# The last of 28 outer products: one inner product leaves PSUM by itself, the last two swap, and the result is stored in halves

## The chip, the cores and the metric

The kernel runs on one core of a Trainium2 chip. The metric is device time in microseconds (us) of one execution; for the kernel before, three runs gave a median of 528.67 (528.14 to 529.69). A separate execution was profiled; lower is better.

## The reference, cut to what matters

`x` holds 64 sequences of 64 tokens, 1024 wide, so 4096 tokens. Two residual layers follow each other.

```python
# layer 0: a low-rank adapter picked by sequence (rank 16)
x = x + einsum('bnr,bor->bno', einsum('bni,bri->bnr', x, B[ids0]), A[ids0])
# layer 1: a dense product and two of eight low-rank experts by token
base   = einsum('btd,od->bto', x, W)
logits = einsum('btd,ed->bte', x, Wr) + 5.0 * one_hot(ids1)
gates  = softmax of the two largest logits, spread over the eight experts
lora   = einsum('bter,bte,eor->bto', einsum('btd,erd->bter', x, A1), gates, B1)
x = x + base + 2.0 * lora
```

All is float32. The kernel adds the identity to W, so that the second residual comes out of the dense product, and works on transposed arrays: `outT` is 1024 outputs by 4096 tokens.

## The kernel before, in words

**Two levels of a product by sevenths.** The dense product takes most of the time. The tokens are cut into eight blocks of 512, and two neighbouring blocks, `ka` and `kb`, make one of four rounds (`s` = 0 to 3, `NSUP` is 4). In a round, the 1024 x 1024 weight matrix and the tokens of the two blocks are each seen as 2 x 2 quarters, and the product of the two is formed from seven products of quarters and sums of them, in place of eight (the method of Strassen and Winograd). These seven are the *outer products*, numbered 1 to 7 and worked in the order `ORDER = (1, 2, 6, 7, 5, 3, 4)` (line 247); the last outer product of the kernel is thus n = 4 of round 3. Each outer product is again formed from seven *inner products*, called p1 to p7 here. Except for two outer products of round 0, all go this way.

**An inner product.** `product(n, ps, k, start)` (line 833) issues four matmuls of 128 x 128 weights by 256 tokens into one PSUM tile of 128 x 2 x 256[...]. For n and k both out of 2, 3, 4 and 7, two more matmuls add the expert part from `b1_sb`. Each float32 matmul shows as two instructions in the profile, so an inner product has 8 or 12 rows there.

**Banks.** Two PSUM tags, `a` and `b`, have two banks each. Within an outer product, p1, p6, p5 and p3 accumulate in one bank of tag `a` (`("pa", s, n)`), in this order; p2 has a bank of tag `b` for itself; p7 and p4 share a further bank of tag `b` (`("pb2", s, n)`).

**How results leave.** The inner sums of this method have terms in common, so a bank is read while it is still being accumulated: `leave(n, ps, i, cs, js, more)` (line 866) reads the bank in its current state and writes it into row half `i` and token half `j` of the outer product's result, in SBUF. Without `more` it adds a stored base (`U` or `V`, sums of earlier outer products; where there is none, ScalarE copies), with `more` it adds to what is there. For n = 4 all are additions on VectorE (DVE) of 128 x 512 elements, with `V` as base. In `step` (line 940), p7 does not leave at once: after p5 there are two additions into the same place (row half 1, token half 1), one of the bank of p1 + p6 + p5 and one of p7's bank. Later p4 is accumulated onto p7, and p4 + p7 is added at row half 1, token half 0.

**The order of the inner products.** The loop in `products` (lines 962 to 986) calls, for each outer product, p1, p2, p6, p7, p5, and keeps p3 and p4 as `rest`, which are put among the first steps of the next outer product: the third after its p1, the fourth after its p2. The last outer product of a round has no successor, so its `rest`, p3 and then p4, ends the round.

**Stores.** `done(n, i, cs, js)` (line 892) is called after p2, p5, p3 and p4, when one token half of one row half is complete. It counts the halves of a row half in `left`; when the second is there, it plans one transfer of the row half, 256 outputs by 512 tokens, 512 KB, on SP's queue.

**What sets the order.** Steps are added to a `Plan` (line 34) with an engine, an estimated duration, what they read and write, a due time `at` and the PSUM or SBUF slots that they take. `Plan.order` runs a simple model of the engines and picks, of the steps that could start first, the one with the smallest due time. The resulting list is issued in that order on each engine, and is not rearranged afterwards. Semaphore waits are put in by the framework, for a PSUM bank by the whole tile: a matmul that writes a bank waits until an earlier read of it is over.

Of the kernel before, what the change touches and what calls it, by code (L numbers as in the profile page):

```python
# [14 lines left out]
P = 128  # L15
# [162 lines left out]
def kernel(  # L178
# [52 lines left out]
    TB = 512  # L231
    NBLK = NT // TB
    NSUP = NBLK // 2
# [5 lines left out]
    QO = O // 4  # L239
    HT = TB // 2  # L240
# [6 lines left out]
    ORDER = (1, 2, 6, 7, 5, 3, 4)  # L247
# [5 lines left out]
    act, pool, sp = Pinned(tc, nc.scalar), Pinned(tc, nc.gpsimd), Pinned(tc, nc.sync)  # L253
# [6 lines left out]
    plan = Plan(slots, {"l"})  # L260
# [25 lines left out]
    half = const.tile([P, 1], F32, name="half")  # L286
# [19 lines left out]
    b1_sb = const.tile([P, O], F32, name="b1_sb")  # L306
# [470 lines left out]
    def products(s):  # L777
        ka, kb = 2 * s, 2 * s + 1
# [9 lines left out]
        def at():  # L788
            return s * SLOTS + slot[0]
# [5 lines left out]
        def q(d, i, cs, js):  # L795
            t = made[d][i] if isinstance(d, str) else made["o", s, d, i]
            return t[:, cs[0] : cs[-1] + 1, js[0] * HT : (js[-1] + 1) * HT]

        def qk(d, i, cs, js):
            return [(name(d, i), c, j) for c in cs for j in js]  # L800

        ALL = (0, 1)

        def whole_product(n, i, c):

            ps, tag = ("pw", s, n, i, c), "ab"[c]
            oh = {2: 0, 3: 0, 7: 1, 4: 1}.get(n)

            def fn(e):
                made[ps] = new(tag, [P, QC, HT], f"pw_{s}_{n}{i}{c}")  # L810
                out = made[ps].rearrange("p c t -> p (c t)")
                mm = [
                    (made[m_q[n][i, j]][:, cc, c * P : (c + 1) * P], made[tokens[n]][:, j * QC + cc])
                    for j in range(2)
                    for cc in range(QC)
                ]
                if oh is not None:
                    o = (oh * 2 + i) * QC + c
                    mm.append((b1_sb[:, o * P : (o + 1) * P], made[whole_h[n]]))
                for x, (lhs, rhs) in enumerate(mm):  # L820
                    pe.matmul(out, lhs, rhs, start=(x == 0), stop=(x == len(mm) - 1))

            reads = [(m_q[n][i, j],) for j in range(2)] + part(tokens[n])
            if oh is not None:
                reads += [("b1",), (whole_h[n],)]
            plan.add(
                {"PE": 3.45 + 0.87 * (oh is not None)}, fn, reads, [(ps,)], at(), [(tag, ps)]
            )
            leave(n, ps, i, (c,), ALL)
            done(n, i, (c,), ALL)  # L830
            slot[0] += 2

        def product(n, ps, k, start):
            last = hd[n][k] if n in (2, 3, 7, 4) and k in (2, 3, 7, 4) else None
            sw, (tx, tk) = wt[n][k], ti[n][k]
            row = {2: 0, 3: 0, 7: 1, 4: 1}.get(k)
            oh = {2: 0, 3: 0, 7: 1, 4: 1}.get(n)

            def fn(e):
                if start:  # L840
                    tag = "a" if k == 1 else "b"
                    made[ps] = new(tag, [P, QC, HT], f"p{tag}_{s}_{n}{k}")
                for j in range(QC):
                    mm = [(made[sw][:, c, j * P : (j + 1) * P], tx()[:, c]) for c in range(QC)]
                    if last is not None:
                        o = (oh * 2 + row) * QC + j
                        mm.append((b1_sb[:, o * P : (o + 1) * P], last[0]()))
                    for c, (lhs, rhs) in enumerate(mm):

                        pe.matmul(  # L850
                            made[ps][:, j, :],
                            lhs,
                            rhs,
                            start=(start and j == 0 and c == 0),
                            stop=(c == len(mm) - 1),
                            skip_group_check=True,
                        )

            reads = [(sw,)] + tk + ([("b1",), last[1]] if last is not None else [])
            plan.add(  # L860
                {"PE": 1.75 + 0.87 * (last is not None)}, fn, reads, [(ps,)], at(),
                [("a" if k == 1 else "b", ps)] * start,
            )
            slot[0] += 1

        def leave(n, ps, i, cs, js, more=False):

            d = dest[n]
            src = d if more else base[n]
            fresh = d == n and cs[0] == 0 and js[0] == 0 and not more  # L870

            def fn(e):
                if fresh:
                    made["o", s, n, i] = new("o", [P, QC, TB], f"o{n}_{s}_{i}")
                out, ins = q(d, i, cs, js), made[ps]
                if len(cs) == 1:
                    ins = ins.rearrange("p c t -> p (c t)").unsqueeze(1)
                if src is None:
                    act.copy(out, ins)
                else:  # L880
                    dve.tensor_tensor(out, ins, q(src, i, cs, js), ALU.add)

            reads = [(ps,)] + (qk(src, i, cs, js) if src is not None else [])

            if d == n and not fresh:
                reads.append((name(d, i), 0, 0))
            plan.add(
                {"ACT": 0.6} if src is None else DVE, fn, reads, qk(d, i, cs, js), at() - 4,
                [("o", name(d, i))] * fresh,
            )  # L890

        def done(n, i, cs, js):

            if n == 5:

                p5, u, v = (lambda d=d: q(d, i, cs, js) for d in (5, "U", "V"))
                k5, ku, kv = (qk(d, i, cs, js) for d in (5, "U", "V"))
                plan.add(
                    DVE, lambda e: dve.tensor_tensor(u(), u(), p5(), ALU.add), ku + k5, ku,
                    at() - 2, sb=True,  # L900
                )
                plan.add(
                    DVE, lambda e: dve.tensor_tensor(p5(), v(), p5(), ALU.add), kv + k5, k5,
                    at() - 2, sb=True,
                )
            oh, k = {2: (0, ka), 5: (1, kb), 3: (0, kb), 4: (1, ka)}.get(n, (None, None))
            if oh is None:
                return
            left[n, i] = left.get((n, i), 2) - 1
            if left[n, i] == 0:  # L910
                o0 = (oh * 2 + i) * QO

                def store(e):
                    sp.dma_start(
                        outT[o0 : o0 + QO, k * TB : (k + 1) * TB].rearrange("(c p) t -> p c t", p=P),
                        made["o", s, n, i],
                    )

                plan.add({"SP": 0.1}, store, qk(n, i, ALL, ALL), [], at() + 2, kb=512)
# [20 lines left out]
        def step(n, k):  # L940
            i, j = {1: (0, 0), 2: (0, 0), 6: (1, 0), 7: (1, 1), 5: (1, 1), 3: (0, 1), 4: (1, 0)}[k]
            if k in (1, 6, 5, 3):
                ps = ("pa", s, n)
                product(n, ps, k, k == 1)
                leave(n, ps, i, ALL, (j,))
                if k == 5:
                    leave(n, ("pb2", s, n), 1, ALL, (1,), True)
            elif k == 2:
                product(n, ("pc", s, n), 2, True)
                leave(n, ("pc", s, n), 0, ALL, (0,), True)  # L950
            else:
                product(n, ("pb2", s, n), k, k == 7)
                if k == 4:
                    leave(n, ("pb2", s, n), 1, ALL, (0,), True)
            if k in (2, 5, 3, 4):
                done(n, i, ALL, (j,))
# [4 lines left out]
        rest = []  # L961
        for n in ORDER:
            after = ORDER[ORDER.index(n) + 1] if n != ORDER[-1] else None
            if (s, n) in WHOLE:
                for k in rest:
                    step(*k)
                rest = []
                for x in range(4):
                    whole_product(n, x // 2, x % 2)
                    if x == 1 and after is not None:  # L970
                        begin(after)
                continue
            step(n, 1)
            if rest:
                step(*rest[0])
            step(n, 2)
            if rest:
                step(*rest[1])
            if after is not None:
                begin(after)  # L980
            step(n, 6)
            step(n, 7)
            step(n, 5)
            rest = [(n, 3), (n, 4)]
        for k in rest:
            step(*k)

# [85 lines left out]
```

## Time and profile before

| what | value |
|---|---|
| median of three runs | 528.67 us (528.14 to 529.69) |
| the profiled execution's own time | 528.18 us |
| its span in the profile | 526.4 us |
| TensorE matmuls (PE) busy | 507.3 us, 96% of the span |
| VectorE (DVE) busy | 290.1 us, 55% |
| GpSimd (POOL) busy | 182.8 us, 35% |
| ScalarE (ACT) busy | 41.1 us, 8% |
| bytes moved by DMA | 99.19 MB, 188 GB/s over the span |
| granted TensorE clock, mean over the span | 0.998 |

The span runs from the first instruction to the last one of the profiled execution. The execution's time has 1.78 us more, which lie around the span. PE rows are matmuls, PEld rows are the loading of their weights, which overlaps them. An instruction's row gives its start, its duration, its engine, the tile it writes and those it reads, and in brackets how long its engine had been idle before it and what it waited for. Almost all instructions are issued through a helper and carry its line, L29, so tiles tell them apart: `pa` and `pb` are tiles of the two PSUM tags, `s` are weights, `t` and `ti` sums of tokens, `he` and `hd` gate values, `o` results, `v` the stored base. The compiler's closing instructions carry line L1069. "SPq" is the queue of SP, which issues the transfers.

### The profile page before, as it was taken

How to read it: one execution, taken by the hardware profiler on the slowest of the kernel's cores; microseconds unless marked ns; L12 is line 12 of the kernel's file. 1: busy time of each engine (PE TensorE's matmuls, PEld its weight loads, DVE VectorE, ACT ScalarE, POOL GpSimd, SP SyncE). 2: the span in 40 equal slices, each digit the busy share in tenths (PEclk: the TensorE clock that was granted, in tenths of full speed). 3: DMA queues.
4: the chain of work that ended last, by engine and by line, in shares of the span. 5: the costliest groups of instructions: out<-in, count | busy, mean ns of one | idle time of the engine just before them, and what ended most of it. 6: DMA issues, size and time to landing. Idle time of an engine off the chain costs nothing.

```text
span 526.4 us, 8463 instructions
## 1 busy us (share of the span) xinstructions
PE 507.3 (96%) x3400; PEld 433.9 (82%) x3400; DVE 290.1 (55%) x554; ACT 41.1 (8%) x81; POOL 182.8 (35%) x149
## 2 busy tenths in 40 slices
PE   2899999999999999999999999999999999999995
PEld 1755768798888988898888998889888898888884
DVE  0639999948964174616674355345567417432632
ACT  1111010002000100011000100000200010001000
POOL 3231955762343234222333313312422323433200
PEclk9999999999999999999999999999999999999999
DMA  8999735768666249735566526743546633610222
GB/s 291 362 364 401 273 135 189 271 226 305 217 202 210 82 113 321 262 106 184 177 190 207 184 82 212 268 159 122 164 161 197 207 92 103 216 42 1 80 81 80
DMA packets 53687, 99.19 MB, mean 188 GB/s; under 512 B 4880, under 2 KB 10000, under 8 KB 53648
## 3 DMA queue, kind: packets, MB, share of 16 engines
q1 hardware_dynamic: 51344, 90.26, 51.6%
q0 software_dynamic: 2304, 8.39, 4.4%
q8 instruction: 27, 0.44, 0.4%
q14 instruction: 12, 0.10, 0.0%
HBM read 69.01 MB, written 29.62 MB: 187 GB/s over the span
## 4 chain that ended last, share of the span: by engine, by line
PE 95%; DMA 2%; DVE 1%; issue 1%; SPq 0%; ACT 0%
PE pa L29 37%; PE pb L29 36%; PE ph L29 11%; PE pw L29 6%; PE px L29 3%; DMA ids_sb<-in_ids 2%; PE pt L29 1%; PE pg L29 1%; SPq L29 0%; DVE o L29 0%; DVE bias L29 0%; ACT o L29 0%; DVE lang L29 0%; DVE bx L29 0%
## 5 line engine op out<-in xcount | busy, mean ns | idle before, releaser
L29 PE MATMUL pa<-ti,s 128*128 128x256 f32 x416 | 99.0, 381 | 0.7 <-ACT o L29 0.7
L29 PE MATMUL pb<-ti,s 128*128 128x256 f32 x376 | 93.4, 380 | 0.0
L29 PEld LDWEIGHTS pa<-ti,s 128*128 128x128 f32 x416 | 77.6, 190 | 12.1 <-ACT o L29 1.1
L29 PEld LDWEIGHTS pb<-ti,s 128*128 128x128 f32 x376 | 70.7, 190 | 9.5
L29 POOL TENSOR_TENSOR ti<-x,ti 128x512 f32<-128x512 f32 x28 | 37.1, 1326 | 85.3 <-PE pb L29 84.3
L29 PEld LDWEIGHTS ph<-a_sb,x 128*128 128x128 f32 x512 | 62.7, 190 | 3.8 <-issue 2.7
L29 PE MATMUL ph<-a_sb,x 128*128 128x136 f32 x512 | 63.3, 279 | 2.1 <-issue 2.1
L29 POOL TENSOR_TENSOR ti<-t,ti 128x512 f32<-128x512 f32 x24 | 33.5, 1396 | 87.3 <-PE pb L29 64.9
L29 POOL TENSOR_TENSOR ti<-x 128x512 f32<-128x512 f32 x26 | 34.1, 1310 | 53.0 <-PE pb L29 31.6
L29 DVE TENSOR_TENSOR o<-pb,o 128x512 f32<-128x512 f32 x45 | 31.0, 690 | 34.1 <-PE pb L29 20.6
L29 PE MATMUL pa<-x,s 128*128 128x256 f32 x208 | 49.8, 379 | 0.0
L29 DVE TENSOR_TENSOR x<-px,x 128x512 f32<-128x512 f32 x64 | 39.8, 682 | 10.4 <-PE px L29 6.1
L29 POOL TENSOR_TENSOR ti<-t 128x512 f32<-128x512 f32 x22 | 29.4, 1339 | 44.1 <-PE pb L29 34.5
L29 PEld LDWEIGHTS pa<-x,s 128*128 128x128 f32 x208 | 38.7, 190 | 4.8
L29 PE MATMUL pa<-t,s 128*128 128x256 f32 x168 | 41.3, 382 | 0.8 <-DVE o L29 0.8
L29 PEld LDWEIGHTS pa<-t,s 128*128 128x128 f32 x168 | 31.4, 190 | 5.7 <-DVE o L29 1.2
L29 DVE TENSOR_TENSOR o<-pa,u 128x512 f32<-128x512 f32 x28 | 19.3, 691 | 26.8 <-PE pa L29 26.3
L29 PE MATMUL pw<-x,w 128*128 128x512 f32 x64 | 28.7, 595 | 0.0
L29 DVE TENSOR_TENSOR u<-pb,u 128x512 f32<-128x512 f32 x21 | 14.5, 689 | 25.5 <-ACT u L29 20.7
L29 PE MATMUL pb<-hg,b_sb 128*128 128x256 f32 x88 | 26.2, 379 | 0.0
L29 DVE TENSOR_TENSOR o<-pa,v 128x512 f32<-128x512 f32 x16 | 11.0, 690 | 27.3 <-PE pa L29 24.7
L29 PE MATMUL pb<-x,s 128*128 128x256 f32 x96 | 23.9, 381 | 0.0
(112 smaller groups left out, 578.9 us busy)
## 6 DMA issues: line engine op xcount, KB each, us to landing
s<-s_kept SPq DMA_DIRECT2D x147, 256.0 KB, 2.7
x<-in_xT SPq DMA_DIRECT2D x16, 1024.0 KB, 5.8
out_T<-o SPq DMA_DIRECT2D x32, 512.0 KB, 3.3
s_kept<-s SPq DMA_DIRECT2D x28, 256.0 KB, 3.8
s_kept<-w SPq DMA_DIRECT2D x18, 256.0 KB, 5.0
w<-in_w SPq DMA_DIRECT2D x16, 256.0 KB, 9.8
s_kept<-m SPq DMA_DIRECT2D x3, 256.0 KB, 5.1
a_sb<-in_a SPq DMA_DIRECT2D x1, 512.0 KB, 14.0
```

Of the source, the lines that this page charges most:

```text
L29: return self._tc.keep_in_program_order(f(*args, **kwargs))
```

## The change

It touches the last outer product (round 3, n = 4) alone. A new helper `last(n)` tells it apart, and the variable `last` of `product` is renamed `extra`. Three things follow for that outer product.

1. p7 leaves by itself, right after it is computed: the bank with p7 is added to `V`, into row half 1, token half 1. After p5 there is then one addition, of p1 + p6 + p5, onto that.
2. The inner order ends p5, p4, p3 where it ended p5, p3, p4.
3. Each token half of a row half is stored when it is complete, 256 outputs by 256 tokens, 256 KB: four transfers in place of two. A contiguous piece in `outT` is then 1 KB long where it was 2 KB.

```diff
+        def last(n):
+            return (s, n) == (NSUP - 1, ORDER[-1])
...
             oh, k = {2: (0, ka), 5: (1, kb), 3: (0, kb), 4: (1, ka)}.get(n, (None, None))
             if oh is None:
                 return
+            o0 = (oh * 2 + i) * QO
+            if last(n):
+
+
+                def half(e):
+                    t0 = k * TB + js[0] * HT
+                    sp.dma_start(
+                        outT[o0 : o0 + QO, t0 : t0 + HT].rearrange("(c p) t -> p c t", p=P),
+                        q(n, i, ALL, js),
+                    )
+
+                plan.add({"SP": 0.1}, half, qk(n, i, ALL, js), [], at() + 2, kb=256)
+                return
             left[n, i] = left.get((n, i), 2) - 1
             if left[n, i] == 0:
-                o0 = (oh * 2 + i) * QO
...
                 product(n, ps, k, k == 1)
-                leave(n, ps, i, ALL, (j,))
-                if k == 5:
+                leave(n, ps, i, ALL, (j,), k == 5 and last(n))
+                if k == 5 and not last(n):
                     leave(n, ("pb2", s, n), 1, ALL, (1,), True)
...
                 product(n, ("pb2", s, n), k, k == 7)
+                if k == 7 and last(n):
+                    leave(n, ("pb2", s, n), 1, ALL, (1,))
                 if k == 4:
                     leave(n, ("pb2", s, n), 1, ALL, (0,), True)
...
-            rest = [(n, 3), (n, 4)]
+            rest = [(n, 4), (n, 3)] if last(n) else [(n, 3), (n, 4)]
```

On the engines, the matmuls of p4 move ahead of those of p3, the five additions of this stage on DVE stay five with the second and third in the new roles, and SP has two transfers more. Everything earlier in the program keeps its place.

More of the change, by code (lines that the diff above doesn't have):

```diff
@@ L833, in product @@
         def product(n, ps, k, start):
-            last = hd[n][k] if n in (2, 3, 7, 4) and k in (2, 3, 7, 4) else None
+            extra = hd[n][k] if n in (2, 3, 7, 4) and k in (2, 3, 7, 4) else None
             sw, (tx, tk) = wt[n][k], ti[n][k]
@@ L844, in fn @@
                     mm = [(made[sw][:, c, j * P : (j + 1) * P], tx()[:, c]) for c in range(QC)]
-                    if last is not None:
+                    if extra is not None:
                         o = (oh * 2 + row) * QC + j
-                        mm.append((b1_sb[:, o * P : (o + 1) * P], last[0]()))
+                        mm.append((b1_sb[:, o * P : (o + 1) * P], extra[0]()))
                     for c, (lhs, rhs) in enumerate(mm):
@@ L857, in fn @@
                         )
-            reads = [(sw,)] + tk + ([("b1",), last[1]] if last is not None else [])
+            reads = [(sw,)] + tk + ([("b1",), extra[1]] if extra is not None else [])
             plan.add(
-                {"PE": 1.75 + 0.87 * (last is not None)}, fn, reads, [(ps,)], at(),
+                {"PE": 1.75 + 0.87 * (extra is not None)}, fn, reads, [(ps,)], at(),
                 [("a" if k == 1 else "b", ps)] * start,
```

## The prediction

> **What bounds the kernel now.** I read the page first: busy shares, then the chain of waits.
>
> ```profile
> PE 507.3 (96%) x3400; PEld 433.9 (82%) x3400; DVE 290.1 (55%) x554; ACT 41.1 (8%) x81; POOL 182.8 (35%) x149
> PE 95%; DMA 2%; DVE 1%; issue 1%; SPq 0%; ACT 0%
> ```
>
> TensorE is busy for 96% of the span and makes 95% of the chain that ends last. An edit pays only by taking a gap out of PE, or by shortening what follows PE's last matmul. The change touches the last outer product alone, so I next read the chain from 495 us to the end.
>
> ```profile
> 513.60 1.74 PE pa L29 x8
> 515.34 0.02 issue
> 515.36 0.70 DVE o L29
> 516.07 0.04 issue
> 516.11 2.86 PE pa L29 x12
> 518.97 2.60 PE pb L29 x12
> 521.57 0.02 issue
> 521.59 0.69 DVE o L29
> ```
>
> The columns are start, duration and what ran. The rows are p5, DVE's read of its bank, p3 into the same bank, p4, and DVE's last addition. PE stands still while DVE reads the bank after p5. The timeline of the same stretch has it as idle time:
>
> ```profile
> 513.44 1.89 PE L29 MATMUL pa<-ti,s 128*128 128x256 f32 x8
> 515.36 0.69 DVE L29 TENSOR_TENSOR o<-pa,v 128x512 f32<-128x512 f32 x1 [3.63 <-PE pa L29]
> 516.11 1.13 PE L29 MATMUL pa<-t,s 128*128 128x256 f32 x4 [0.78 <-DVE o L29]
> ```
>
> After the last addition only the store is left: first the transfers from `o` between 505 and 527 us, then what SP's closing instructions waited for.
>
> ```profile
> L29 SPq DMA_DIRECT2D out_T<-o x4: 372/372/373, 504.9 to 522.3; - x4
> DMA to landing us min/median/max: 2.7/2.7/2.8
> ```
> ```profile
> SPq L1069 <- DMA out_T<-o: 2.3, 1, 2.3
> ```
>
> The last 512 KB store is issued at 522.3 us and lands 2.7 us later, at 525.0. The closing instructions fill the remaining 1.4 us to 526.4.
>
> [...]here PE restarts 0.06 us after the read ends (516.05 to 516.11). [...]The trace has 690 to 692 for these additions, and the new ones have the same shape. [...]Here the last store's packets run from 523.2 to 524.7 us, which leaves 2.7 - 1.5 = 1.2 us outside them[...]. [...]In the packet records of this trace a 1 KB packet (the 4096 of the loads of W) takes 49 ns at the median and a 2 KB one 84, not the 98 of two 1 KB packets[...].
>
> **The change, part by part.**
>
> *The swap, p4 ahead of p3.* PE's steady pace is that of p7: 12 instructions from 510.85 to 513.44, 0.216 us each. p5's eight need 8 x 0.216 = 1.73, so p3 was due at 513.44 + 1.73 = 515.17. It started at 516.11, 0.94 late. Its restart is slow as well: its 12 take 2.69 (516.11 to 518.80) where 12 at pace take 2.59. The stall is worth 0.94 + 0.10 = 1.04 us. After the change p4 follows p5 in another bank, at 515.17. p3 then comes at 515.17 + 2.59 = 517.76, long after the read of its bank ended at 516.05: cover 1.65 us after the semaphore's 0.06. PE ends at 521.56 - 1.04 = 520.52. If that cover were gone, up to 1.04 comes back.
>
> *p7 leaves alone.* This makes the swap possible: before, p7's bank was read only at 516.09 to 516.78, with p5's, so p4 directly behind p5 would have waited still longer. Now DVE reads it after p7's last row ends, 513.59, so from 513.61 to 514.30. p4 may write it from 514.36 and is due at 515.17: 0.81 us of cover. DVE is idle then (the 3.63 us in its row). The count of additions stays five, at 0.69 each, so the cost is nothing. Queued behind this addition on DVE is only p5's, which cannot start before 515.34.
>
> *What p4 needs 3.6 us earlier* (515.17 instead of 518.80). Its weights are in the last load, issued at 461.8 us; the loads of that stretch land in at most 3.4. Its token sum is POOL's last instruction, over at 495.16, and its gate difference ended on DVE at 450.8. None comes near.
>
> *Four half stores.* SP issues two more transfers, 0.37 us each, in a stretch in which it waits for DVE for 11.4 us: free. The four go out at 507.42 (after p2), 516.07 (p5), 518.65 (p4) and 521.26 (p3). The first is ahead of the previous outer product's store, due at 510.01, and delays nothing. The third's packets run from 0.9 after its issue, as the last store's did, to about 520.5. The last's begin at about 522.2, so they don't meet. Completion slots of older transfers that they reuse are 50 us old or more, or, for the stores, over 10.
>
> *The last store.* It is 256 KB instead of 512, but of 1 KB pieces: still 256 packets, 16 for each of 16 DMA engines. By the medians, 16 x 84 = 1.34 us becomes 16 x 49 = 0.78, so it saves 0.56 and lands in 2.1. This trace has no store in 1 KB pieces, so I bound it. Below: 256 KB stores in 2 KB pieces, in a calmer stretch at 104 to 106 us, land in 2.0 at the best. Above: the time goes by packets alone and 2.7 stays.
>
> ```profile
> L29 SPq DMA_DIRECT2D s_kept<-s x2: 319/320/320, 104.6 to 105.8; - x2
> DMA to landing us min/median/max: 2.0/2.7/3.4
> ```
>
> The 3.4 is a transfer behind others. I take 2.1, a saving of 0.6, with 0 to 0.7 as its ends. Nothing follows the store but the closing instructions, so what it saves is time.
>
> **Sum.** PE's end 520.52; DVE 520.54 to 521.23; issue 521.26; landing 523.36; closing 1.4: span 524.76, which is 526.4 - 1.04 - 0.6. With the 1.78 us around the span the profiled execution would be 528.18 - 1.64 = 526.54. The median of the three runs, 528.67, lies 0.49 above the profiled run, and one of the three, 529.69, is far from the other two. From the median the sum gives 527.03. I forecast 526.9, a little under it, since the profiled run and the lowest (528.14) are within 0.04 of each other. That is -0.33%.
>
> **Rivals.**
>
> *A: the half store lands no sooner* (2.7, by packets). For it: 256 packets as before. Against it: 49 against 84 ns. Only the stall is gained: 527.6.
>
> *B: the stall moves to the other bank.* p4 would wait for DVE's read of p7 as p3 did for that of p5. It needs that read to end after 515.11 instead of 514.30, and DVE has been idle since 511.74. If it happened at full price, only the store's 0.6 remains: 528.1.
>
> *C, slower: 1 KB writes into HBM, or their receipt, are far slower than 1 KB reads.* The trace's 1 KB packets are reads of HBM, and a store's receipt for such pieces isn't shown. The price is the last store's landing alone. It makes up the gain of 1.04 when it takes 3.75 us, and costs over 0.3% (1.59 us) from 2.7 + 1.04 + 1.59 = 5.3 us. For it: among the kernel's 32 stores landings reach 8.1. Against it: these have other transfers on the queue, and the last four in the quiet tail all took 2.7 to 2.8. At 5.8 us the time would be 528.67 - 1.04 + 3.1 = 530.7.
>
> *D: the change does not do what it says.* The order in which instructions stand in the changed kernel has p7's addition second on DVE, p4 before p3 on PE, and the halves at SP's end, so only the waits could spoil it; that is B.
>
> **How the numbers follow.** About 0.3% (1.59 us) is what a measurement of this kernel can tell from no change, so "faster" begins at 527.08. The forecast gets 0.76, A 0.12, B 0.06, C 0.04, and 0.02 remain for what I don't see. The forecast's own range is 526.2 to 527.4: the sum from either base (526.54, 527.03), 0.3 below and 0.4 above for scatter of medians and a landing of 2.0 to 2.4. It straddles 527.08, and I give 0.56 of its 0.76 to the faster side; the rest, A and B count as the same. With a share of the remainder: faster 0.57, same 0.38, slower 0.05. The range to hold 8 in 10 takes in A with scatter: 526.2 to 527.9.
>
> **What would show it.** Right: PE shows no idle time between p7 and its last matmul, with p4 directly behind p5; DVE has an addition from `pb` and `v` at about 513.6; DVE's last one reads `pa` and `v` and starts near 520.5; the last store lands about 2.1 us after its issue; the span is 524.5 to 525.0. A: that landing is 2.7. B: idle time before p4, released by DVE. C: a landing above 3.7, with packets much longer than 49 ns. The prediction would also be wrong if the closing instructions took longer than 1.4 us.

## The result, and the profile after

| | before | after |
|---|---|---|
| median | 529.14 us (22 runs, 528.08 to 530.92) | 528.0 us (22 runs, 526.19 to 529.24) |
| ratio to before | | 0.9971, 95% interval 0.9962 to 0.998 |
| profiled execution: its time | 528.18 us | 526.65 us |
| its span | 526.4 us | 524.9 us |

The change makes the kernel faster by 0.29% (0.2 to 0.38). The ratio applied to the median that the forecast started from, 528.67, gives 527.1, where 526.9 was forecast. It is not the quotient of the two medians, which is 0.9978, and the medians lie about a microsecond above the two profiled runs, because each kernel's times fall into two groups some 1.6 us apart; the last section tells what was found of their cause.

The page's busy shares after show that TensorE did the same work in a shorter span:

```profile
PE 507.1 (97%) x3400; PEld 434.6 (83%) x3400; DVE 290.1 (55%) x554; ACT 41.1 (8%) x81; POOL 182.8 (35%) x149
```

The end of the chain of waits after (start, duration, what ran):

```profile
511.27 2.59 PE pb L29 x12
513.86 1.73 PE pa L29 x8
515.59 2.59 PE pb L29 x12
518.18 2.60 PE pa L29 x12
520.78 0.02 issue
520.80 0.69 DVE o L29
```

These are p7, p5, p4 and p3, then DVE's last addition. The DVE piece between p5 and the next inner product is gone, and p4 follows p5 at once. The timeline of this stretch shows where p7's bank is read now:

```profile
513.70 1.89 PE L29 MATMUL pa<-ti,s 128*128 128x256 f32 x8
513.90 0.69 DVE L29 TENSOR_TENSOR o<-pb,v 128x512 f32<-128x512 f32 x1 [1.90 <-PE pb L29]
515.42 1.03 PE L29 MATMUL pb<-ti,s 128*128 128x256 f32 x4
515.63 0.69 DVE L29 TENSOR_TENSOR o<-pa,o 128x512 f32<-128x512 f32 x1 [1.03 <-PE pa L29]
```

DVE reads it from 513.90 to 514.59, while p5 runs in the other bank. p4, which writes it again, starts at 515.42, 0.83 us later; by the forecast's times (514.30 and 515.17) it was 0.87. Last, the half stores (those after 515 us), and the wait of SP's closing instructions:

```profile
L29 SPq DMA_DIRECT2D out_T<-o x3: 372/372/372, 516.3 to 521.5; - x3
DMA to landing us min/median/max: 2.1/2.1/2.1
```
```profile
SPq L1086 <- DMA out_T<-o: 1.6, 1, 1.6
```

Each lands 2.1 us after its issue; the 512 KB stores of before took 2.7.

**A measure for the tail.** Before p7 of the last outer product the change adds one half store, at 507.71, and nothing else. p7 began at 510.85 before and 511.11 after; the same 0.26 us lie between the two at 495 us (an inner product in `pb` starts at 495.31 and 495.57), ahead of all that was changed, so they are chance. So I take the time from p7's first matmul to the end of the span and cut it in four, by the starts of DVE's last addition and of the last store's issue and by the last landing in the trace:

| | to DVE's last addition | to the last issue | to landing | closing | sum |
|---|---|---|---|---|---|
| before | 10.74 | 0.72 | 2.75 | 1.34 | 15.55 |
| after | 9.69 | 0.72 | 2.14 | 1.21 | 13.76 |
| difference | -1.05 | 0 | -0.61 | -0.13 | -1.79 |

The tail is 1.79 us shorter. The profiled spans differ by 1.53, which is 0.26 less, since the profiled execution after came to p7 that much later.

### The profile page after: what moved, and what is told of

The parts are those of the page before. It is cut to its first block, busy times and chain, and to the rows that moved or that the text cites. A ratio compares the mean times of both kernels' runs of the same rounds, so it can differ in the third digit from the quotient of the medians.

```text
span 524.9 us, 8468 instructions
## 1 busy us (share of the span) xinstructions
PE 507.1 (97%) x3400; PEld 434.6 (83%) x3400; DVE 290.1 (55%) x554; ACT 41.1 (8%) x81; POOL 182.8 (35%) x149
## 4 chain that ended last, share of the span: by engine, by line
PE 95%; DMA 2%; issue 0%; DVE 0%; SPq 0%; ACT 0%
PE pa L29 37%; PE pb L29 36%; PE ph L29 11%; PE pw L29 6%; PE px L29 3%; DMA ids_sb<-in_ids 2%; PE pt L29 1%; PE pg L29 1%; SPq L29 0%; DVE bias L29 0%; DVE o L29 0%; ACT o L29 0%; DVE lang L29 0%; DVE bx L29 0%
## 5 line engine op out<-in xcount | busy, mean ns | idle before, releaser
L29 DVE TENSOR_TENSOR u<-pb,u 128x512 f32<-128x512 f32 x21 | 14.5, 689 | 25.5 <-ACT u L29 20.7
L29 DVE TENSOR_TENSOR v<-pa,u 128x512 f32<-128x512 f32 x16 | 11.0, 688 | 22.4 <-PE pa L29 22.4
```

The costliest lines, as they stand in the source:

```text
L29: return self._tc.keep_in_program_order(f(*args, **kwargs))
```

## The experiments

Each kernel was profiled, and its tail is cut like the table above. Ratios are to the kernel before.

### One part alone: the order without the halves, and the halves without the order

The change with whole stores:

```diff
-            if last(n):
+            if False:
```

> The change without its half stores: p7 leaves alone, p4 ahead of p3, and two stores of 512 KB. My theory (gain = stall 1.04 + last store 0.61 + 0.13 in the closing instructions): no idle time on PE after p5, last store lands 2.7 us after its issue, closing 1.35 us as before, so 15.55 - 1.04 = 14.5 us from p7's first matmul to the end of the span (before 15.55, changed kernel 13.76), ratio to before 0.998. Rival (the stall was hidden under the store's traffic and only the store counts): 15.5 us, ratio 1.000.

The end of its chain:

```profile
515.46 1.73 PE pa L29 x8
517.18 2.59 PE pb L29 x12
519.77 2.60 PE pa L29 x12
522.38 0.02 issue
522.40 0.69 DVE o L29
```

There is no stall. The parts are 9.70, 0.72, 2.75 and 1.34, in all 14.51 us, where 14.5 was expected. The stall's 1.04 us is a gain by itself, and store and closing are as before. The ratio, 0.9985 (0.9969 to 1.0), would not settle this alone, since its interval reaches 1; the trace does.

The halves alone, with p7's addition back behind p5's and p3 ahead of p4:

```diff
-                leave(n, ps, i, ALL, (j,), k == 5 and last(n))
-                if k == 5 and not last(n):
+                leave(n, ps, i, ALL, (j,))
+                if k == 5:
...
-                if k == 7 and last(n):
-                    leave(n, ("pb2", s, n), 1, ALL, (1,))
...
-            rest = [(n, 4), (n, 3)] if last(n) else [(n, 3), (n, 4)]
+            rest = [(n, 3), (n, 4)]
```

> The half stores alone, with the old order p5, p3, p4 and p7's addition after p5's. My theory: PE keeps the idle 0.78 us before p3, the last store lands 2.1 us after its issue, and the closing instructions take 1.21 us as in the changed kernel, so 15.55 - 0.61 - 0.13 = 14.8 us from p7's first matmul to the end, ratio 0.9986. Rival (a half store lands early only behind an early PE end, or meets the half before it, issued 2.6 us earlier): lands in 2.7 us or more, 15.5 us, ratio 1.000.

Its timeline has the stall again, and its last three stores land sooner:

```profile
517.54 1.13 PE L29 MATMUL pa<-t,s 128*128 128x256 f32 x4 [0.79 <-DVE o L29]
```
```profile
L29 SPq DMA_DIRECT2D out_T<-o x3: 372/372/373, 518.2 to 523.7; - x3
DMA to landing us min/median/max: 2.1/2.1/2.1
```

The parts are 10.75, 0.72, 2.14 and 1.21, in all 14.81 (expected 14.8). Ratio 0.9985 (0.9971 to 0.9999). The two halves of the change gain 1.04 and 0.74 us, together 1.78 of the 1.79: they add up.

### Which edit removes the stall? Two misses

Then I undid one of the two edits to the order, with the halves kept. First p7's addition back behind p5's, with `rest = [(n, 4), (n, 3)]` as changed:

> The changed kernel with p7's addition put back behind p5's (p4 still ahead of p3, half stores kept). My theory: p4 must wait for two reads, of the bank with p5 (0.69 us) and then of p7's (0.69 us), so PE idles 0.78 + 0.73 = 1.5 us before p4, released by DVE, and none before p3: 13.76 + 1.77 = 15.5 us from p7's first matmul to the end, ratio to before 1.000. Rival (p7 alone is not needed, the swap itself removes the stall): no idle time, 13.8 us, ratio 0.997.

Second the changed kernel with only `rest` set back to p3, p4:

> The changed kernel with p3 ahead of p4 again (p7 leaves alone, half stores kept). My theory: p3 waits for the read of its own bank after p5 as before, 0.78 us idle and 0.1 us of slow restart; p7's early addition gains nothing by itself; 13.76 + 1.04 = 14.8 us from p7's first matmul to the end, ratio 0.9986. Rival (one addition after p5 instead of two releases PE earlier): less than 0.3 us idle, 14.0 us, ratio 0.9972.

Both expectations failed, and so did the first rival; the second one's rival had the missing idle time, but not its cause. The first row is from the timeline of the kernel with p7's addition put back, the second from the chain of the one with `rest` put back:

```profile
516.62 1.13 PE L29 MATMUL pa<-t,s 128*128 128x256 f32 x4 [0.79 <-DVE o L29]
```
```profile
515.86 2.59 PE pb L29 x12
```

In the first kernel p3 (`pa`, 12 rows) still follows p5, although `rest` puts p4 first: its order on every engine is that of the halves alone, and so is its tail, 14.80 us (ratio 0.9983, 0.9972 to 0.9994). In the second, p4 (`pb`) follows p5 although `rest` puts p3 first: it has the changed kernel's instructions in the changed kernel's order, and its tail is 13.76 us (ratio 0.9969, 0.9959 to 0.998). The line with `rest` decides nothing. This fits the planner's rule, to take the step that can start first: with p7 read early that is p4, with p7 read behind p5 it is p3.

So I enforced the orders in the plan, by a read that the planner must respect. p4 ahead of p3, with p7's addition behind p5's:

```diff
             reads = [(sw,)] + tk + ([("b1",), extra[1]] if extra is not None else [])
+            if last(n) and k == 3:
+                reads.append((("pb2", s, n),))
```

> p4 ahead of p3 enforced by a dependency in the plan, half stores kept, but p7's addition put back behind p5's. My theory: p4 waits for two reads on DVE, that of the bank with p5 and then p7's: PE idles 0.78 + 0.73 = 1.5 us before p4 and not at all before p3, and 13.76 + 1.77 = 15.5 us run from p7's first matmul to the end, ratio to before 1.000. Rival (the order alone removes the stall): 13.8 us, ratio 0.997.

Its timeline between p5, which ends at 517.00, and p4:

```profile
517.03 0.69 DVE L29 TENSOR_TENSOR o<-pa,v 128x512 f32<-128x512 f32 x1 [3.63 <-PE pa L29]
517.76 0.69 DVE L29 TENSOR_TENSOR o<-pb,o 128x512 f32<-128x512 f32 x1
518.55 0.67 PE L29 MATMUL pb<-ti,s 128*128 128x256 f32 x2 [1.55 <-issue]
```

The profile names no releaser for p4, but the two reads fill the stall of 1.55 us, and p4 starts 0.10 us after the second ends. The parts are 11.49, 0.72, 2.12 and 1.21, in all 15.54 (expected 15.5), ratio 0.9999 (0.9988 to 1.0011): the order without the early read costs what the halves gain. The other way round, p3 ahead of p4 with p7 read early (`k == 4` and `("pa", s, n)` in the same place, `rest` put back):

> p3 ahead of p4 enforced by a dependency in the plan; p7 leaves alone and the half stores stay. My theory: p3 waits for the read of its own bank after p5, 0.78 us idle and 0.1 us of slow restart as in the kernel before; p7's early addition gains nothing without the other order. 13.76 + 1.04 = 14.8 us from p7's first matmul to the end. Rival (one addition after p5 in place of two releases PE earlier): under 0.3 us idle, 14.0 us.

```profile
516.63 1.13 PE L29 MATMUL pa<-t,s 128*128 128x256 f32 x4 [0.78 <-DVE o L29]
```

Its tail is 14.80 in its one run, as expected. The early read and the order are needed together, and the first brings the second with it.

### What the last store is worth

The half that is complete since p2 is held back, so that both go out at the end:

```diff
+                if i == 0 and js == (0,):
+                    held.append(half)
+                    return
                 plan.add({"SP": 0.1}, half, qk(n, i, ALL, js), [], at() + 2, kb=256)
+                if i == 0:
+                    plan.add({"SP": 0.1}, held[0], qk(n, i, ALL, ALL), [], at() + 2, kb=256)
```

> The changed kernel, but the first token half of row half 0, complete since p2, is sent only behind the last half, so that both 256 KB halves of 1 KB pieces go out at the end. My theory (a store's time is its packets on the 16 engines, 46 ns each, and the gain is that half of them have gone earlier): 2 x 16 x 46 ns = 1.47 us of packets in a row, the second store lands about 0.75 us later than the last store of the changed kernel, and 14.4 to 14.5 us run from p7's first matmul to the end of the span (changed kernel 13.76, before 15.55). Rival (each small store has its own time of 2.1 us from its issue, 0.4 us after the other's): 0.4 us later, 14.1 us.

```profile
L29 SPq DMA_DIRECT2D out_T<-o x2: 372/417/462, 522.1 to 522.5; - x2
DMA to landing us min/median/max: 2.2/2.3/2.5
```

The two land 2.2 and 2.5 us after their issues, which are 0.43 apart, so the second 2.91 after the first issue. The tail is 14.53 us (14.4 to 14.5 was expected, 14.1 by the rival), 0.77 longer than the changed kernel's and within 0.02 of that with whole stores, ratio 0.9985 (0.9975 to 0.9994). Their packets run as one block, 512 of them from 522.98 to 524.65, 46 ns each at the median. So the gain here is that half of the bytes are gone before the end, not that stores are small.

Without the last store:

```diff
+                if i == 0 and js == (1,):
+                    return
                 plan.add({"SP": 0.1}, half, qk(n, i, ALL, js), [], at() + 2, kb=256)
```

> The changed kernel without its last store: the last quarter of the last outer product's result (256 outputs by 256 tokens) is computed but not written out. My theory: the end is then DVE's last addition and the closing instructions, which the last landing no longer holds up: the other half store, issued 2.6 us earlier, lands 0.5 us before DVE ends. 9.7 us from p7's first matmul to PE's end and 0.7 for DVE, plus 0.9 to 1.2 of closing, 11.4 to 11.6 us (changed kernel 13.76), so that the whole store is worth about 2.2 us at the end. Rival (stores are waited for in another way, or the closing has work of its own in parallel): above 12.5 us.

In its one run the tail is 11.35 us, 0.05 under the range. The half before lands 0.4 us ahead of the end of DVE's last addition, and the closing ends 0.96 us behind that. The last store is thus worth 2.41 us: its 2.14 and issue, and 0.25 of the closing, part of which runs during DVE's addition here.

### The closing instructions

The third term, 0.13 us, was not forecast. SP's closing tests the eight completion semaphores of its transfers one after the other, in the same order in every profile. In the profile they are SP's `EVENT_SEMAPHORE` rows, and these are the ones from the last landing on, before and after:

```profile
L1069 SPq EVENT_SEMAPHORE  x8: 28/28/28, 525.1 to 525.5; - x8
L1086 SPq EVENT_SEMAPHORE  x6: 28/28/28, 523.7 to 524.0; - x6
```

The eight start between 525.08 and 525.51, one every 0.06 us. The last store had the first of the eight semaphores before, and with two more transfers it has the third. Five earlier stores of the round were cut in two to move it to the eighth:

```diff
+                if s == NSUP - 1 and (n, i) in ((2, 0), (5, 0), (5, 1), (3, 0), (3, 1)):
+                    for c in ALL:
+                        plan.add(
+                            {"SP": 0.1}, lambda e, c=c: store(e, (c,)), qk(n, i, (c,), ALL), [],
+                            at() + 2, kb=256,
+                        )
+                    return
```

> The changed kernel with five earlier stores of round 3 cut into two of 256 KB, so that five more transfers precede the last one. The closing instructions test the eight completion semaphores of SP's transfers one after the other, 0.06 us each, and the last store then has the eighth in place of the third. My theory: they take 5 x 0.06 = 0.3 us less behind the last landing, 1.21 - 0.31 = 0.9 us, and 13.45 us run from p7's first matmul to the end (changed kernel 13.76). Rival (the closing's 0.14 us between the two kernels is chance, or goes with the number of transfers): 1.2 us or more, 13.76 us or more.

```profile
L1095 SPq EVENT_SEMAPHORE  x1: 28/28/28, 524.0 to 524.0; - x1
```

The parts are 9.69, 0.72, 2.14 and 0.91, in all 13.46 (13.45 expected). One test alone stands behind the last landing here, and the closing takes 1.34, 1.21 and 0.91 us with eight, six and one: 0.06 for each test. The ratio, 0.9975 (0.9964 to 0.9987), says nothing on 0.3 us either way.

### A version beyond the change

p3's first 128 output rows are ready 1.3 us before its second, but both are in one bank. Here the bank is split in two, one of them from the tag `l`; the first half leaves and is stored while PE works on the second. Four earlier stores are cut as above.

```diff
-                if start:
+                if start and two:
+                    for j in range(QC):
+                        made[ps + (j,)] = new("al"[j], [P, 1, HT], f"p{j}_{s}_{n}{k}")
+                elif start:
...
-                            made[ps][:, j, :],
+                            made[ps + (j,)][:, 0, :] if two else made[ps][:, j, :],
...
-                leave(n, ps, i, ALL, (j,), k == 5 and last(n))
+                for c in ALL if last(n) else ():
+                    leave(n, ps + (c,), i, (c,), (j,), k == 5)
+                    if k == 3:
+                        done(n, i, (c,), (j,))
```

> A version beyond the changed kernel: the bank of p1, p6, p5 and p3 of the last outer product is split into two banks by output rows, so that the first half of p3's result leaves and is stored while PE still works on the second; the last addition is 128 x 256 (0.42 us in place of 0.69) and the last store 128 KB. Four earlier stores are cut in two, so that the last store has the eighth completion semaphore. My theory: the last store has 8 packets for each engine in place of 16, lands in 2.14 - 8 x 0.046 = 1.77 us, and the closing takes 0.9: 13.76 - 0.27 - 0.37 - 0.3 = 12.8 us from p7's first matmul to the end, ratio to before 0.995. Rival (a small store has a floor of 2.1 us, and the two banks cost PE a wait): 13.2 us or more, ratio 0.996.

The timeline of its last addition, and its stores after 520 us:

```profile
522.15 0.42 DVE L29 TENSOR_TENSOR o<-p,v 128x256 f32<-128x256 f32 x1 [0.87 <-PE p L29]
```
```profile
L29 SPq DMA_DIRECT2D out_T<-o x3: 344/344/383, 520.3 to 522.6; - x3
DMA to landing us min/median/max: 1.8/1.8/1.8
```

The parts are 9.70, 0.45, 1.79 and 0.91, in all 12.85 (12.8 expected). Six runs have a median of 525.69 us, ratio 0.9944 (0.9923 to 0.9965). In the trace it is 0.91 us better than the change and 2.7 better than before.

### Two attempts on the two groups of times

Twenty-four matmuls of the first block (`px`) were repeated, to keep PE busy in a pause near 19 us:

```diff
+            for _ in range(24 if (k, h) == (0, 1) else 0):
+                pe.matmul(
+                    made[px[gi]][:, c, :],
+                    made["ga", k][strip, cc * P : (cc + 1) * P],
+                    made["bx", k][strip, :],
+                    start=True, stop=True, tile_position=(gi * CG, 0),
+                )
```

> The changed kernel with 24 of its first block's matmuls repeated onto the same values, about 1.5 us of work in the 2.0 us in which PE stands still near 19 us. My theory of the two groups of times, 1.6 us apart: in some executions a 3.41 us window of the clock at 22 us is granted at 0.5, because most of the window before it was idle. With the gap filled no execution has the clock at 0.997; all times lie in the lower group, 526.2 to 527.3, the median near 526.6, ratio to before 0.995. Rival (the lowered window is no consequence of the idle time): both groups remain, median 527 to 528, and the extra matmuls gain nothing.

```profile
16.61 7.43 PE L29 MATMUL px<-bx,ga 32*128 32x128 f32 x112 [0.74 <-DVE bx L29]
```

The ratio is 1.0089 (1.0072 to 1.0107). 64 of these rows take 2.07 us before and 112 take 7.43 here: 0.03 us for a row that goes to the four strips of the array (32 rows each) in turn, and 0.11 for a repeat. The repeats stay on one strip and also write one place, and no run tells which of the two costs the time. DVE then waited 3.88 us for them. This tested nothing of the theory. The second attempt put full-width matmuls ahead of the gate product:

```diff
+                for _ in range(5 if (k, j) == (0, 0) else 0):
+                    pe.matmul(made[ph][:, 0, :P], ident, ident, start=True, stop=True)
```

> The changed kernel with five matmuls of the identity into the tile that the first rows of the gate product overwrite afterwards: about 1.2 us of full-width work in the 2.0 us in which PE stands still near 19 us, between 19.5 and 20.7. Theory of the two groups of times, 1.6 us apart: a 3.41 us window at 22 us is granted half the clock when the window before it holds the whole idle stretch. With it cut to under 1 us no run has the clock at 0.997: all times in the lower group, 526.2 to 527.4, ratio to before about 0.995. Rival (the lowered window is no consequence of the idle time): both groups remain and the ratio stays at 0.997 or above.

```profile
20.84 1.38 PE L29 MATMUL ph<-ident 128*128 128x128 f32 x10 [1.91 <-DVE x L29]
```

They waited for DVE to free the tile, so the pause stayed at 1.9 us and what follows began 0.9 us later (22.05 in place of 21.14). Both groups remain (11 of 16 runs from 527.24 to 527.76, five from 528.72 up, four of them with a mean clock of 0.997), ratio 0.9974 (0.9962 to 0.9986). The pause was not filled in time, so this decides nothing either.

## Why the prediction was right, point by point

- **What bounds it.** Right: the whole gain lies in PE's one gap of the last outer product and in what follows PE's end.
- **The swap, 1.04 us.** The size is right to 0.01: DVE's last addition starts 1.05 us earlier, and 1.04 in the kernel without half stores. That p4 directly behind p5 needs the early read is right too: without it PE stood still for 1.55 us, where it was 0.78 before. What is wrong is that the swap counts as an edit of its own. In fact the line that swaps is without effect in both directions, and the early read alone moves p4 ahead through the planner. The order of the instructions under each edit alone would have shown it.
- **p7 alone, at no cost.** Right: five additions of 0.69, and 0.83 us between p7's read and p4, where the prediction's times give 0.87 (0.81 behind the semaphore's 0.06).
- **p4's inputs, 3.6 us earlier.** Right: PE has no idle time before p4.
- **The last store, 0.6 us.** 0.61 was measured. The step from the 49 ns of 1 KB packets that are read carried over to packets that are written: 46 ns, 256 of them from 522.41 to 523.31. All of the saving is packet time: from issue to the first packet it is 0.89 us in both kernels, from the last packet to the landing 0.35. Landing in 2.1 us was right.
- **The closing, 1.4 us in both.** The saving here was put at nothing and is 0.13: the closing takes 1.34 before and 1.21 after. The two added transfers were costed on SP's queue alone. They also move the last store's place among the completion semaphores, which the closing tests in turn.
- **The sum.** 1.64 us forecast, 1.79 in the tail, 1.53 between the profiled executions, whose stretch before p7 is 0.26 us longer after, and 1.53 by the ratio. That the ratio comes so close to the forecast is in part luck: the forecast misses 0.13 in the closing, and the measured gain is held down because more of the runs after (14 of 22, against 11) fall into the upper group.
- **The base and the range.** The prediction set 529.69 apart from the other two runs as a stray. It is one of an upper group that holds half of the 22 runs before, so 0.3 or 0.4 us for the scatter of a median was too little: the median after, 528.0, lies above both stated ranges, as the one before lies above 528.67. So the comparison goes by the ratio.
- **The rivals.** A and C fall with the 2.14 us landing, B with the missing stall before p4. What C feared, a slow receipt for 1 KB pieces, isn't there: 0.35 us from the last packet to the landing, as with 2 KB pieces.
- **The chances.** The ratio is 0.9971 and its interval straddles 0.997, where the prediction put the bar; "faster" had 0.57 and "same" 0.38.

## What to carry to other kernels

At the end of a kernel, read the tail as a sum (last gap on the busiest engine, last addition, issue, packets, landing, closing) and send everything that is complete before the last piece: here the packet time still to go set the landing (256 packets in both kernels, but of 46 ns where they took 84), and two small stores sent together at the end gained nothing (a tail of 14.53 us against 14.51 with one whole store). A bank read between two accumulations stalled the busiest engine here by 0.78 us, for a read of 0.69. With p4 between the two, p3 had no idle time before it, and the early read of p7's bank freed p4 for that place. Where a planner orders the steps, an edit's program order says little, so it pays to read the resulting instruction order of every edit alone.

## What the runs showed that I had not expected

**The closing's semaphore tests.** 0.06 us for each test behind the last landing; with eight, 0.43 us hang on which semaphore the last transfer has.

**A lowered clock that comes and goes.** The 22 runs of the change split into 8 from 526.19 to 527.19 with a mean granted clock of 1.0 and 14 from 527.78 to 529.24 with 0.997; their medians, 526.48 and 528.12, are 1.64 us apart. The 22 runs before split into two groups of 11, at 528.42 and 529.95. Group against group the change gains 1.94 and 1.83 us, near the 1.79 of the tail; against the runs before of their own session, whole stores gain 1.09 and 1.12, halves alone 0.83 and 0.85 (tails 1.04 and 0.74). Why the shares of the groups differ is not known. A profile of the upper kind (the change with whole stores) has a stretch of 3.41 us at half the clock near 22 us, which the profile of the kernel before lacks. By stages (duration, busy times, granted clock, DMA share, GB/s), first that kernel, then before:

```profile
18.68:22.09 3.41, 1.37 (x24) 1.21 (x18) 3.34 (x7) 0.00 (x0) 0.94 (x1) 1.00 1.04 375
22.09:25.50 3.41, 3.41 (x17) 3.41 (x17) 3.34 (x8) 0.00 (x0) 0.00 (x0) 0.50 1.05 394
```
```profile
18.99:22.40 3.41, 1.67 (x14) 1.70 (x15) 3.41 (x7) 0.00 (x0) 0.94 (x1) 1.00 1.03 374
22.40:25.81 3.41, 3.41 (x32) 3.41 (x31) 3.34 (x8) 0.97 (x2) 0.42 (x1) 1.00 1.04 396
```

PE pauses for 2 us near 19 to 21 us in nearly all of these kernels. The clock's changes lie on a grid of 3.41 us that starts at another point in each execution: the traces have the full clock on record from 15.57 to 524.16 us before and from 16.18 to 524.77 after, 508.59 us in both, which is 149 steps of 3.413. In the five profiles with the lowered stretch, the interval of the grid just before it holds 2.0 us of PE idle time or more (2.00, 2.02, 2.04, 2.04, 3.14). In the nine without, none there holds more than 1.85, since the grid cuts the pause or the pause is shorter. The end of the program fits: in 13 of the profiles the clock falls to half after the first interval with 2.60 us or more of PE idle time behind the last matmuls, and never after one with 1.49 or less. No matmul follows it there, and the 2.24 us at half the clock up to the end of the span (524.16 to 526.40) are why the kernel before has a mean clock of 0.998. In the lowered stretch above PE has 17 rows where it has 32 at the full clock. By an estimate from its length and clock, 3.41 x 0.5, such a stretch costs 1.7 us, and the groups are 1.64 apart. This is a pattern in 14 profiles, and no experiment shows it as the cause, since both that meant to fill the pause missed it. If it holds, over half of the executions of the change (14 of 22) lose about as much there as the change gains.
